# Two graph attention layers: the last products of each layer rearranged, the overflow count moved into layer 1, one early load moved forward

## The chip, the cores and the metric

The kernel runs on one core of a Trainium2 chip. The metric is the device time of one execution in microseconds (us), lower is better; the figure for a kernel is the median of its runs. Profiles are one execution each, taken by the hardware profiler. A core has five engines with a queue of instructions each: TensorE (PE, with its weight loads PEld), VectorE (DVE), ScalarE (ACT), GpSimd (POOL) and SyncE (SP). An engine works its queue off in order; engines wait for each other on semaphores.

## The reference

There are 2708 nodes with 1024 features each, `x`, and an adjacency matrix `adj` with some 16 entries that count in each row. Two layers follow each other, each with a residual and a layer norm without weights:

```python
# layer 0
f = x @ Wf + bf;  g = x @ Wg + bg
e = relu(f @ g.T)
attention = softmax(where(adj > 0, e, NEG), axis=1)
x = layernorm(x + attention @ (x @ W + bW))
# layer 1
h = x @ W1;  f1 = h @ a1;  f2 = h @ a2
e = leaky_relu(f1 + f2.T, 0.2)
attention = softmax(where(adj > 0, e, NEG), axis=1)
x = layernorm(x + relu(attention @ h))
```

## The kernel before

**Lists.** The first 225 us read `adj` and make of each row a list of its at most 40 neighbours, in four columns of up to 10 (`SL`). The nodes are sorted by the length of their lists into 85 groups of 32, and the groups stand in 22 blocks: block 0 has one group (20 valid nodes), the others four each (128 nodes). The table `TILES` says how many gathers each group gets, 3 to 10; a tile is one gather of 128 rows: for 32 nodes, one neighbour of each of the four columns. Over all groups there are 405 tiles. If a node of the input has more neighbours than its group has tiles for, the lists don't fit, and the kernel must take another path; that is what the overflow table `over` is for: it marks the places of `SL` beyond each group's tiles, and a valid neighbour in a marked place sets `flag`. The flag is loaded into the engines' registers at the end (`values_load`, L1065), and a branch (L102) jumps to `general_path` if it is set. With this input it is not.

**Reordered algebra.** Layer 0 takes M = Wf Wg^T once, so that the score of a node and its neighbour is a dot of the row `F = x M` with the neighbour's own `x`. The neighbours' `x` are gathered, weighted sums are made of them, and only then the sum is multiplied by `W` (`Wt`). Layer 1 likewise: it gathers rows of a table T, which holds the layer norm's output and beside it, in column D, that row's product with `u2 = W1 a2`; its score needs no dot, only that column and `f1`.

**A block in layer 0** (loop over `units`, in the order 1, 0, 2, 3, ..., 21). `lay.gathers` (L645) issues indirect DMAs on POOL into a ring of 20 slots, as soon as a slot is free. `f_product` is 32 matmuls of 128x512 and two short ones for the bias, on PE (`product`, L533, and `half_product`, L541). `replicate` copies F on ACT into the four `Fr` tiles. `dots` makes one DVE instruction with 1024 elements a tile. `soft` (L806 and L652) is the softmax on DVE, with its exponential on ACT; it ends with `st`, the weights spread for PE, and `rs`, the row sums. `sums` (L682) runs the weighted sums on PE into the PSUM tile `po`, whose scaled copy is `y`. `turn` (L515) transposes y on PE in eight steps, yields, and then copies the transposes on ACT to `yT`. `product` with `Wt` makes the last matrix product of the block in a PSUM tile `pm`. `close` (L817) adds the residual, computes mean and variance and three Newton steps for the inverse root on DVE (`norm`, L585), scales on ACT, stores the rows to X1S (SP), makes the two dots with `u1b` and `u2b` on DVE and scatters the row with its extra column into T (POOL). `load_residual` (L811) gathers the block's own x into the tile `zs`, which there is once; for the last block it goes into a ring slot.

The work is staggered over the loop: in the turn of block b, PE runs the sums of b, then the product of the block before with `Wt`, then F of a block ahead, then the transposes of y of b; the closing of the block before that is spread over the same turn as a generator of four pieces. All these engines are wrapped in `InOrder`, so program order is queue order. The PSUM pool `ps_m` has two buffers, each of two banks of 512 columns: F and the products with `Wt` take turns in them.

**Layer 1** goes over blocks 0 to 21 in that order with a ring of 32 slots (`ring` and `more`). Its turn has gathers from T, scores (`scores1`), softmax, sums, transposes, a product with `M`, now W1, and `close1` (L1001): relu, residual from X1S, norm, scatter to the output. After the loop come the last product, two closings, and then the overflow table: 88 memsets on POOL, three DVE instructions, a matmul and a copy to `flag`.

**At the start** x of block 1 and 0 and the lists of these blocks are gathered first, then the 15 tiles of block 1 (`lay.most`, L846), then x of block 2 (`load_x(2)`), then further lists.

Of the kernel before, what the change touches and what calls it, by code (L numbers as in the profile page):

```python
# [8 lines left out]
F32 = mybir.dt.float32  # L9
# [97 lines left out]
def listed_path(ctx, tc, x, adj, Wf, bf, Wg, bg, W, bW, W1, a1, a2, out):  # L107
# [433 lines left out]
    def half_product(pm, h, n, xT, w, row=None):  # L541
# [3 lines left out]
        for k in range(KC):  # L545
            pe.matmul(pm[:n, h, :], xT[:, k, :n], w[:, k, c],
                      start=(row is None and k == 0), stop=(k == KC - 1))

    def split_product(xT, w, parts, row=None):

        pm = ps_m.tile([P, H, 512], F32, name="pm")
        for h in range(H):
            c = slice(h * 512, (h + 1) * 512)
            if row is not None:
                pe.matmul(pm[:32, h, :], ones3[row:row + 3, :32], rows3[row:row + 3, c], start=True, stop=False)
            for k in range(KC // Q):
                for p in range(Q):
                    i = p * KC // Q + k  # L560
                    pe.matmul(pm[32 * p:32 * p + 32, h, :], xT[:, i, :32], w[:, i, c],
                              start=(k == 0 and (row is None or p > 0)), stop=(k + 1 == KC // Q))
        act.copy(parts, flat(pm))
        yield
        pm = ps_m.tile([P, H, 512], F32, name="pm")
        for h in range(H):
            pe.matmul(pm[:, h, :], rep, parts[:, h * 512:(h + 1) * 512], start=True, stop=True)
        return pm
# [13 lines left out]
            out=table, out_offset=bass.IndirectOffsetOnAxis(ap=idx, axis=0), in_=src,  # L582
            in_offset=None, bounds_check=N - 1, oob_is_err=False)

    def norm(z, n):  # L585


        st = small.tile([P, H, 6], F32, name="bst")
        mv = small.tile([P, 2], F32, name="mv")
        for h in range(H):  # L590
            dve.bn_stats(st[:n, h, :], z[:n, h * 512:(h + 1) * 512])
        dve.bn_aggr(mv[:n], st[:n])
        var, r, t = (small.tile([P, 1], F32, name=s) for s in ("var", "rstd", "newton"))
        dve.tensor_scalar(var[:n], mv[:n, 1:2], EPS, None, op0=ALU.add)
        ri, ti = r.bitcast(I32), t.bitcast(I32)
        dve.tensor_scalar(ti[:n], var.bitcast(I32)[:n], 1, None, op0=ALU.logical_shift_right)
        dve.tensor_scalar(ri[:n], ti[:n], -1.0, float(0x5F3759DF), op0=ALU.mult, op1=ALU.add)
        for _ in range(3):
            dve.tensor_scalar(t[:n], var[:n], r[:n], r[:n], op0=ALU.mult, op1=ALU.mult)
            dve.tensor_scalar(t[:n], t[:n], -0.5, 1.5, op0=ALU.mult, op1=ALU.add)  # L600
            dve.tensor_scalar(r[:n], r[:n], t[:n], None, op0=ALU.mult)
        sh = small.tile([P, 1], F32, name="sh")
        dve.tensor_scalar(sh[:n], mv[:n, 0:1], r[:n], -1.0, op0=ALU.mult, op1=ALU.mult)
        yield
        act.activation(z[:n, :D], z[:n, :D], AF.Identity, bias=sh[:n], scale=r[:n])
# [141 lines left out]
    with ExitStack() as s0s:  # L747
# [69 lines left out]
        def close(b):  # L817

            n, m, z = nrows[b], valid[b], Z.pop(b)
            dve.tensor_add(z[:n, :D], flat(Wp.pop(b))[:n], z[:n, :D])  # L820
            steps = norm(z, n)
            next(steps)
            yield
            for _ in steps:
                pass
            sp.dma_start(X1S[start[b]:start[b] + m, :], z[:m, :D])
            yield
            dot(z[:n, :D], u1b, n, f1[:n, b:b + 1])
            dot(z[:n, :D], u2b, n, z[:n, D:D + 1])
            yield  # L830
            if z is not zs:
                pool.memset(z[:, D + 1:], 0.0)
            scatter(T1[:, :], ids[:m, b:b + 1], z[:m])
# [9 lines left out]
        load_lists(0)  # L843
        q_dot(1)
        q_dot(0)
        lay.most = len(units[0].tiles)  # L846
        first_gathers(1, 5)
        x_turn(1)
        spread0, spread1 = q_spread(0), q_spread(1)
        next(spread1)  # L850
        load_x(2)
        load_lists(2)
        lay.most += len(units[1].tiles)
        first_gathers(0, 1)
        x_turn(0)

        halves, xT = [], xTs.pop(1)
        for h in range(H):
            halves.append(ps_m.tile([P, H, 512], F32, name="pm"))
            half_product(halves[h], h, P, xT, M, 0)  # L860
        pool.memset(zs[:, D:], 0.0)
        load_lists(3)
        next(spread0)
# [27 lines left out]
        for k, u in enumerate(units):  # L891
# [18 lines left out]
            next(closing, None)  # L910
            for r in reps[1:3]:
                replicate(nxt.b, r)
            lay.sums(u, po, {12: [lambda s=closing: [None for _ in s]]}, y[b])
            closing = iter(())
            if ahead is not None and not first:
                x_turn(ahead)
            if k + 3 < NB and not first:
                loaded = seq[k + 3]
                load_x(loaded)
            if back is not None:  # L920
                load_residual(back)
                if back > 0:
                    Wp[back] = product(P, yTs.pop(back)[0], Wt, 32)
                else:
                    Wp[back] = whole(split_product(yTs.pop(back)[0], Wt, frp.tile([P, D], F32, name="Fr"), 32))
# [11 lines left out]
            steps = turn(y[b], nrows[b], yT, halves=True)  # L937
            next(steps)
            yTs[b] = yT, steps
            if k + 4 < NB and not first:  # L940
                load_lists(seq[k + 4])
            if nxt is not None:
# [9 lines left out]
        load_residual(b)  # L952
        for _ in yTs[b][1]:
            pass
        Wp[b] = product(nrows[b], yTs.pop(b)[0], Wt, 32)
        for _ in closing:
            pass
        for _ in close(b):
# [3 lines left out]
    with ExitStack() as s1s:  # L962
# [38 lines left out]
        def close1(b):  # L1001
            m, xt, z = valid[b], x1[b % 2], z1[b % 2]
            sp.dma_start(xt[:m], X1S[start[b]:start[b] + m, :])
            dve.scalar_tensor_tensor(z[:m], flat(prod.pop(b))[:m], 0.0, xt[:m], op0=ALU.max, op1=ALU.add)
            for _ in norm(z, m):
                pass
            yield
            scatter(out, ids[:m, b:b + 1], z[:m])

        lay.gathers()  # L1010
        scores1(units[0])
        closing = iter(())
        waiting = []
        for k, u in enumerate(units):
            nxt = units[k + 1] if k + 1 < len(units) else None
            b = u.b
            back = b - 1 if b > 0 else None
            po = ps_s.tile([P, H, 512], F32, name="po")
            y[b] = yp.tile([P, D], F32, name="y1")
            if back is not None:  # L1020
                for _ in yTs[back][1]:
                    pass
            lay.sums(u, po, {6: [lambda s=closing: [None for _ in s]]}, y[b])
            closing = iter(())
            if back is not None:
                if back > 0:
                    prod[back] = product(P, yTs.pop(back)[0], M)
                else:
                    prod[back] = whole(split_product(yTs.pop(back)[0], M, z1[1]))
            yT = tp.tile([P, KC, P], F32, name="yT")  # L1030
            steps = turn(y.pop(b), nrows[b], yT, halves=True)
            next(steps)
            yTs[b] = yT, steps
            if waiting:
                closing = close1(waiting.pop())
                next(closing)
            if back is not None:
                waiting.append(back)
            if nxt is not None:
                scores1(nxt)  # L1040
        for _ in closing:
            pass
        b = NB - 1
        for _ in yTs[b][1]:
            pass
        prod[b] = product(nrows[b], yTs.pop(b)[0], M)
        for b in waiting + [b]:
            for _ in close1(b):
                pass


        over = ovp.tile([P, NG, QT], F32, name="over")
        pool.memset(over, 0.0)
        for g in range(1, NG):
            if TILES[g] < QT:
                pool.memset(over[:, g, TILES[g]:], 1.0)
        for q in range(Q):
            pool.memset(over[32 * q:32 * q + valid[0], 0, TILES[0]:], 1.0)
        dve.scalar_tensor_tensor(over, SL, float(N), over, op0=ALU.is_lt, op1=ALU.mult)
        dve.tensor_reduce(bad[:, 0:1], over, AX.XY, ALU.add)  # L1060
        dve.tensor_reduce(bad[:, 0:1], bad, AX.X, ALU.add)
        pt = ps_t.tile([P, 4, P], F32, name="pt")
        pe.matmul(pt[0:1, 0, 0:1], bad[:, 0:1], ones, start=True, stop=True)
        act.copy(flag, pt[0:1, 0, 0:1])
    return nc.values_load(flag[0:1, 0:1])  # L1065


@with_exitstack
def general_path(
# [360 lines left out]
```

## Time and profile before

| | us |
|---|---|
| median of 3 runs | 1803.02 |
| lowest, highest | 1797.66, 1807.29 |
| span of the profiled execution | 1799.5 |
| lists, and the first gathers of x | 0 to about 228 |
| layer 0, first matmul of a block to the last scatter to T | 228 to 1177 |
| layer 1, first gather from T to the last scatter of the output | 1177.6 to 1786.4 |
| overflow table, flag and the end of the program | 1786.4 to 1799.5 |

Busy over the whole span: PE 1573.3 us (87%), DVE 1172.8 (65%), POOL 1187.0 (66%), ACT 636.4 (35%). These shares are means over stages with different limits. A line of the timeline reads: start in us from the span's start, length in us, engine, line of the kernel (L71 is the wrapper `InOrder`, so nearly all lines name it; go by the tiles), operation, output tile <- input tiles, shape, how many were merged, and in brackets the engine's idle time ahead of it and what ended that. In a table by stage each engine's busy time stands with its count. POOL's 0.3 us between two DMA issues is shown as idle time that "issue" ended.

### The profile page before, as it was taken

How to read it: one execution, taken by the hardware profiler on the slowest of the kernel's cores; microseconds unless marked ns; L12 is line 12 of the kernel's file. 1: busy time of each engine (PE TensorE's matmuls, PEld its weight loads, DVE VectorE, ACT ScalarE, POOL GpSimd, SP SyncE). 2: the span in 40 equal slices, each digit the busy share in tenths (PEclk: the TensorE clock that was granted, in tenths of full speed). 3: DMA queues.
4: the chain of work that ended last, by engine and by line, in shares of the span. 5: the costliest groups of instructions: out<-in, count | busy, mean ns of one | idle time of the engine just before them, and what ended most of it. 6: DMA issues, size and time to landing. Idle time of an engine off the chain costs nothing. (4 is left out here: it accounts for less than half of the span.)

```text
span 1799.5 us, 22910 instructions
## 1 busy us (share of the span) xinstructions
PE 1573.3 (87%) x7313; PEld 669.9 (37%) x7313; DVE 1172.8 (65%) x3537; ACT 636.4 (35%) x861; POOL 1187.0 (66%) x1191
## 2 busy tenths in 40 slices
PE   5999279899999999999999997828989889889995
PEld 3544124343444443444444443303333333333332
DVE  4879737888888888888888887422442433433442
ACT  5545354444445545445554444101111111111110
POOL 7888476567666666766666653067777777777741
PEclk9999679899999999999999998959999999999997
DMA  7747068568777777777777786189999999999960
GB/s 267 262 151 261 20 238 303 209 211 292 292 262 263 261 262 260 278 276 287 289 293 275 260 292 227 71 339 368 362 394 393 393 360 396 392 391 381 370 229 26
DMA packets 149982, 501.86 MB, mean 279 GB/s; under 512 B 32565, under 2 KB 32597, under 8 KB 147144
## 3 DMA queue, kind: packets, MB, share of 16 engines
q0 software_dynamic: 132032, 427.36, 64.2%
q1 hardware_dynamic: 10202, 55.72, 8.2%
q10 hardware_dynamic: 7618, 17.23, 2.7%
q8 instruction: 59, 0.97, 0.2%
q14 instruction: 71, 0.58, 0.1%
HBM read 509.64 MB, written 33.75 MB: 302 GB/s over the span
## 5 line engine op out<-in xcount | busy, mean ns | idle before, releaser
L71 POOL DMA_INDIRECT ring<-in_x_dram,SL x405 | 439.9, 1086 | 258.2 <-issue 97.9
L71 DVE SCALAR_TENSOR_TENSOR j<-ring,Fr 128x1024 bf16<-128x1024 f32 x402 | 495.2, 1232 | 81.8 <-DMA ring<-in_x_dram,SL 55.6
L71 ACT COPY Fr<-pm 32x1024 f32<-32x1024 f32 (+2 forms) x353 | 340.7, 965 | 21.0 <-PE pm L71 16.3
L71 PE MATMUL po<-ring,st 128*32 128x512 f32 x2660 | 340.6, 619 | 0.1
L71 POOL DMA_INDIRECT ring<-T,SL x260 | 259.4, 998 | 84.9 <-issue 57.2
L71 PE MATMUL pm<-M,xT 128*128 128x512 f32 (+1 forms) x704 | 311.5, 622 | 0.4 <-ACT xT L71 0.4
L71 PE MATMUL pm<-Wt,xT 128*128 128x512 f32 (+1 forms) x704 | 303.5, 599 | 0.0
L71 PE MATMUL pm<-M,yT 128*128 128x512 f32 (+1 forms) x704 | 298.5, 595 | 0.3 <-ACT yT L71 0.3
L71 ACT ACTIVATE scores<-scores 128x24 f32<-128x24 f32 (+5 forms) x44 | 9.8, 222 | 667.7 <-DVE scores L71 667.7
L71 PEld LDWEIGHTS pm<-M,xT 128*128 128x128 f32 (+1 forms) x704 | 127.3, 191 | 172.1 <-issue 171.4
L71 PEld LDWEIGHTS pm<-M,yT 128*128 128x128 f32 (+1 forms) x704 | 127.2, 186 | 170.2 <-issue 169.7
L71 PEld LDWEIGHTS pm<-Wt,xT 128*128 128x128 f32 (+1 forms) x704 | 125.0, 186 | 151.8 <-issue 151.6
L71 POOL DMA_INDIRECT more<-T,SL x145 | 144.7, 998 | 44.6 <-issue 32.6
L71 PEld LDWEIGHTS po<-ring,st 128*32 128x32 f32 x2660 | 104.9, 115 | 185.6 <-issue 182.4
L71 DVE TENSOR_SCALAR scores<-ring,f1q 128x2 f32<-128x2 f32 (+5 forms) x98 | 21.7, 241 | 209.9 <-DMA ring<-T,SL 208.3
L409 POOL TENSOR_TENSOR adj<-adj,iota 128x2708 f32<-128x2708 f32 (+3 forms) x23 | 130.5, 5686 | 21.5 <-ACT adj L71 21.4
L71 ACT ACTIVATE y<-po,ri 128x512 f32<-128x512 f32 (+1 forms) x88 | 55.9, 684 | 221.4 <-PE po L71 203.9
L412 DVE MAX8 cand<-adj 128x8 f32<-128x136 f32 (+2 forms) x440 | 96.6, 285 | 36.3 <-POOL adj L409 36.3
L71 PE MATMUL pt<-rs,stack 128*32 128x1 f32 x680 | 13.8, 177 | 118.0 <-DVE rs L71 68.8
L71 PE MATMUL pm<-halfT,WfT 128*128 128x512 f32 x256 | 112.5, 594 | 1.5 <-ACT WfT L71 1.5
L71 POOL DMA_INDIRECT SL<-LD,idq x85 | 86.0, 1012 | 25.8 <-issue 20.9
L71 PE MATMUL po<-more,st 128*32 128x512 f32 x580 | 91.7, 639 | 0.0
(198 smaller groups left out, 1411.9 us busy)
## 6 DMA issues: line engine op xcount, KB each, us to landing
adj<-in_adj_dram SPq DMA_DIRECT2D x21, 1354.0 KB, 6.0
X1S<-z SPq DMA_DIRECT2D x20, 512.0 KB, 6.3
ring<-in_x_dram,SL POOLq DMA_INDIRECT x405, 6.4
u1b<-X1S SPq DMA_DIRECT2D x11, 512.0 KB, 7.1
rb<-X1S SPq DMA_DIRECT2D x10, 512.0 KB, 7.2
ring<-T,SL POOLq DMA_INDIRECT x260, 7.3
rows<-in_L_gnn_Wg_dram ACTq DMA_DIRECT2D x8, 512.0 KB, 6.4
rows<-in_L_gnn_Wf_dram ACTq DMA_DIRECT2D x8, 512.0 KB, 3.4
```

What stands on the lines that cost most here:

```text
L71: made = self.tc.keep_in_program_order(op(*args, **kwargs))
L409: nc.gpsimd.tensor_tensor(k[:n, cut], k[:n, cut], iota[:n, cut], op=ALU.mult)
L412: nc.vector.max(cand[:n, s, :], k[:n, s * SEG:min((s + 1) * SEG, N)])
```

## The change

It has four parts, all about the ends of the layers and one about the beginning.

1. Layer 0, last turn: the product of block 20 with `Wt` is queued ahead of the last sums instead of after them. For that its yT is copied out at the end of turn 20 already, ahead of the softmax of block 21 on ACT's queue, and what is left of the closing of block 19 and the residual of block 20 come first. The purpose is to give PE work while it waits for the last softmax.
2. The last product of both layers goes into two PSUM tiles of the pool instead of one, so that the add and the statistics of the first 512 columns can run while PE makes the second. In `close` the dot with `u2b`, which the scatter needs, is put ahead of that with `u1b`.
3. The overflow table is filled, eight memsets a turn, during the first eleven turns of layer 1; it is counted in the turn of block 12, and the flag is loaded at the end of the turn of block 20. It is to leave nothing but the branch for the end of the kernel.
4. At the start, x of block 2 is gathered after half of the tiles of block 1, so that the work on it can start sooner.

```diff
+    def two_products(n, xT, w, row=None):
+        halves = [ps_m.tile([P, H, 512], F32, name="pm") for h in range(H)]
+        for h in range(H):
+            half_product(halves[h], h, n, xT, w, row)
+        return halves
...
-    def norm(z, n):
+    def norm(z, n, made=None):
...
         for h in range(H):
+            if made is not None:
+                made(h)
             dve.bn_stats(st[:n, h, :], z[:n, h * 512:(h + 1) * 512])
...
         def close(b):
-            dve.tensor_add(z[:n, :D], flat(Wp.pop(b))[:n], z[:n, :D])
-            steps = norm(z, n)
+            pm = Wp.pop(b)
+            def add(h):
+                c = slice(h * 512, (h + 1) * 512)
+                dve.tensor_add(z[:n, c], pm[h][:n, h, :], z[:n, c])
+            if b + 1 < NB:
+                dve.tensor_add(z[:n, :D], flat(pm)[:n], z[:n, :D])
+            steps = norm(z, n, None if b + 1 < NB else add)
...
+            dot(z[:n, :D], u2b, n, z[:n, D:D + 1])
             dot(z[:n, :D], u1b, n, f1[:n, b:b + 1])
-            dot(z[:n, :D], u2b, n, z[:n, D:D + 1])
...
-        lay.most = len(units[0].tiles)
+        lay.most = len(units[0].tiles) // 2
         first_gathers(1, 5)
...
         load_x(2)
+        lay.most = len(units[0].tiles)
+        lay.gathers()
         load_lists(2)
...
+            if nxt is None:
+                for _ in closing:
+                    pass
+                load_residual(back)
+                Wp[back] = product(P, yTs.pop(back)[0], Wt, 32)
             lay.sums(u, po, {12: [lambda s=closing: [None for _ in s]]}, y[b])
...
-            if back is not None:
+            if back is not None and nxt is not None:
                 load_residual(back)
...
             yTs[b] = yT, steps
+            if k + 2 == NB:
+                for _ in steps:
+                    pass
...
-        Wp[b] = product(nrows[b], yTs.pop(b)[0], Wt, 32)
+        Wp[b] = two_products(P, yTs.pop(b)[0], Wt, 32)
...
         lay.gathers()
+        pool.memset(over, 0.0)
         scores1(units[0])
...
+            if k == NB // 2 + 1:
+                count_over()
             lay.sums(u, po, {6: [lambda s=closing: [None for _ in s]]}, y[b])
...
+            for i in (2 * k, 2 * k + 1):
+                if i < NB:
+                    mark_over(i)
+            if k + 2 == NB:
+                unfit = nc.values_load(flag[0:1, 0:1])
...
-        prod[b] = product(nrows[b], yTs.pop(b)[0], M)
+        prod[b] = two_products(P, yTs.pop(b)[0], M)
```

`close1` gets the same `add(h)` as `close`, with its relu in it; `mark_over(b)` holds the memsets of a block's groups, and `count_over` the three DVE instructions, the matmul and the copy to `flag` that stood at the end. The old block at the end is gone.

More of the change, by code (lines that the diff above doesn't have):

```diff
@@ L855, in listed_path @@
         x_turn(0)
[L857 to L860, printed above, removed]
+        halves = two_products(P, xTs.pop(1), M, 0)
         pool.memset(zs[:, D:], 0.0)
@@ L1003, in close1, with add @@
             sp.dma_start(xt[:m], X1S[start[b]:start[b] + m, :])
-            dve.scalar_tensor_tensor(z[:m], flat(prod.pop(b))[:m], 0.0, xt[:m], op0=ALU.max, op1=ALU.add)
-            for _ in norm(z, m):
+            pm = prod.pop(b)
+            def add(h):
+                c = slice(h * 512, (h + 1) * 512)
+                dve.scalar_tensor_tensor(z[:m, c], pm[h][:m, h, :], 0.0, xt[:m, c], op0=ALU.max, op1=ALU.add)
+            if b + 1 < NB:
+                dve.scalar_tensor_tensor(z[:m], flat(pm)[:m], 0.0, xt[:m], op0=ALU.max, op1=ALU.add)
+            for _ in norm(z, m, None if b + 1 < NB else add):
                 pass
@@ L1008, in close1, with mark_over, count_over @@
             scatter(out, ids[:m, b:b + 1], z[:m])
+        over = ovp.tile([P, NG, QT], F32, name="over")
+        def mark_over(b):
+            for g in groups[b]:
+                if g == 0:
+                    for q in range(Q):
+                        pool.memset(over[32 * q:32 * q + valid[0], 0, TILES[0]:], 1.0)
+                elif TILES[g] < QT:
+                    pool.memset(over[:, g, TILES[g]:], 1.0)
+        def count_over():
+            dve.scalar_tensor_tensor(over, SL, float(N), over, op0=ALU.is_lt, op1=ALU.mult)
+            dve.tensor_reduce(bad[:, 0:1], over, AX.XY, ALU.add)
+            dve.tensor_reduce(bad[:, 0:1], bad, AX.X, ALU.add)
+            pt = ps_t.tile([P, 4, P], F32, name="pt")
+            pe.matmul(pt[0:1, 0, 0:1], bad[:, 0:1], ones, start=True, stop=True)
+            act.copy(flag, pt[0:1, 0, 0:1])
         lay.gathers()
+        pool.memset(over, 0.0)
         scores1(units[0])
@@ L1049, in listed_path @@
                 pass
[L1052 to L1065, printed above, removed]
+    return unfit
 @with_exitstack
```

## The prediction

> **What bounds the kernel now.** I read four views, in this order: the page's list of costly groups, to see which engine is full where; the busy table by stage; and then the instructions in order of time at the three places that the change touches (start of layer 0, seam between the layers, end of the kernel).
>
> First, the stages. Columns: stretch, its length, busy time of PE, PEld, DVE, ACT and POOL with counts, granted clock, DMA share, GB/s.
> ```profile
> 282.00:1111.00 829.00, 795.12 (x3556) 335.86 (x3556) 713.79 (x1600) 414.92 (x499) 544.29 (x509) 0.99 0.75 269
> 1111.00:1178.00 67.00, 41.31 (x155) 16.47 (x154) 32.94 (x93) 7.48 (x12) 6.56 (x8) 0.81 0.26 93
> 1178.00:1705.00 527.00, 449.96 (x2541) 185.37 (x2542) 193.60 (x813) 69.72 (x135) 403.13 (x405) 0.94 0.99 381
> ```
> Layer 0 (first row) is TensorE: 795 of 829 us. The seam (second row) is 67 us in which nothing is full: a chain. Layer 1 (third row) looks like DMA (0.99), but 403 us of POOL in 405 instructions are 1.0 us each, and 0.30 us of issue lie ahead of each: 405 x 1.30 = 526 us of 527. So POOL's gather issue has no free slot there, and the DMA queue behind it is full too. The groups of that stage show the 0.30 us: 245 gathers, 77.9 us idle before them.
> ```profile
> L71 POOL DMA_INDIRECT ring<-T,SL x245 | 244.2, 997 | 77.9 <-issue 50.9 <-DMA ring<-T,SL 9.8 <-PE po L71 3.7
> ```
> Second, the seam in order of time (start, length, engine, what, idle time before and its releaser):
> ```profile
> 1110.07 1.04 PE L71 MATMUL pt<-ident,y 128*128 128x128 f32 x8
> ...
> 1121.05 0.22 ACT L71 ACTIVATE scores<-scores 128x16 f32<-128x16 f32 x1 [13.56 <-DVE scores L71]
> 1121.29 1.14 ACT L71 COPY xT<-pt 128x512 f32<-128x512 f32 x3
> ...
> 1122.25 0.39 PE L71 MATMUL pt<-rs,stack 128*32 128x1 f32 x16 [11.14 <-DVE rs L71]
> ...
> 1122.46 9.90 PE L71 MATMUL po<-ring,st 128*32 128x512 f32 x60
> ...
> 1136.12 1.03 POOL L71 DMA_INDIRECT z<-in_x_dram,ids  x1 [2.65 <-DMA T<-z,ids]
> ...
> 1147.16 1.23 DVE L71 TENSOR_TENSOR z<-pm,z 128x1024 f32<-128x1024 f32 x1 [15.41 <-PE pm L71]
> ...
> 1162.79 1.22 DVE L71 TENSOR_TENSOR ring<-pm,ring 128x1024 f32<-128x1024 f32 x1 [5.98 <-PE pm L71]
> ...
> 1173.37 1.00 POOL L71 DMA_INDIRECT T<-ring,ids  x1 [14.63 <-DVE fq L71]
> ...
> 1177.61 1.03 POOL L71 DMA_INDIRECT ring<-T,SL  x1 [3.24 <-DMA T<-ring,ids]
> ```
> The reader is to see that PE stands still for 11.14 us before the last sums while the transposed y of block 20 lies ready in PSUM, that its copy out waits behind the softmax on ACT's queue, and that two products of 14.8 us then follow the sums one after the other. The first gather of layer 1 hangs on the end of that chain.
>
> Third, the end of the kernel:
> ```profile
> 1778.00 1.23 DVE L71 SCALAR_TENSOR_TENSOR z<-pm,u1b 128x1024 f32<-128x1024 f32 x1 [9.38 <-PE pm L71]
> ...
> 1785.39 0.97 POOL L71 DMA_INDIRECT out_dram<-z,ids  x1 [14.25 <-ACT z L71]
> 1786.36 4.18 POOL L71 MEMSET over<- 128x850 f32 x88
> ...
> 1793.25 0.15 ACT L71 CAST flag<-pt 1x1 int32<-1x1 f32 x1 [8.13 <-PE pt L71]
> ```
> Last, the start, where x of block 2 is used:
> ```profile
> 254.96 0.58 PE L71 MATMUL pm<-rows,ones 3*32 3x512 bf16 x1 [9.21 <-ACT Fr L71]
> ...
> 255.33 1.23 DVE L71 SCALAR_TENSOR_TENSOR j<-xb,rb 128x1024 bf16<-128x1024 f32 x1 [9.32 <-DMA xb<-in_x_dram,ids]
> ...
> 281.56 0.31 PE L71 MATMUL pt<-rs,stack 128*32 128x1 f32 x16
> ```
>
> [...] after the 11.14 us gap the clock is 0.5 until 1128.2, and the 60 sums take 9.90 us where 64 take 7.05 us at 1088.42. [...] 1.0 us of POOL for each gather, so POOL work in layer 1 is not free. [...] the flag's loads take 0.46 to 0.54 us here.
>
> **Part by part.**
>
> x of block 2 sooner. Its gather (248.98) goes ahead of 8 of the 15 gathers of unit 0, 8 x 1.3 = 10.4 us. DVE's first dots can start when ACT's copies of Fr are there, about 250.2, not 256.97: DVE is 6.8 us earlier. But PE waits at 254.96 for ACT's copies, then runs the small product, the transposes and the product of block 2 without a pause to 281.35, and the sums follow at 281.56; rs was ready at 280.25. So the gain lies beside PE: **0** (0 to 1).
>
> Product of block 20 ahead of the last sums, with its y copied out early. Block 21's own case shows transposes to product as 1146.96 to 1147.93 = 0.97 us, so product 20 starts at 1111.0 and ends 14.8 us later, 1125.9. Its PSUM buffer was F of block 21, free since 1107.5. rs of unit 21 is ready at 1122.1, hence the sums start at 1125.9, at full clock: 60 x 0.110 + 0.4 = 7.0, end 1132.9. Now y, transposes and copies of block 21 are bare, as product 20 no longer hides them: unit 0 shows 289.17 to 291.24 = 2.1 us. Product 21 runs from 1135.0 to 1149.8, in place of 1162.75.
>
> Two PSUM tiles, and the other queue. The second half of product 21 takes the buffer that DVE's add of block 20 empties, a new wait. That add needs x in z, whose gather follows the scatter of block 19. With u2b's dot first, that scatter goes 1.27 us sooner: 1131.2; gather 3.7 later, 1134.9; landing 4.2 later (as at 1136.12), 1139.1; the add is over at 1140.4, the first half of product 21 at 1142.4. The wait is covered by 2 us. DVE goes on with block 20: add to shift 5.8 us (1147.16 to 1153.0), ACT 1.3, two dots 2.5: 1148.7. Then the halves of block 21, 0.62 + 0.65 each: the first is hidden until 1150.0, the second ends at 1151.3. Before, 1165.3: **14.0 us**. The dots' order gives the last scatter another **1.3** (it waits for u2b's dot at 1172.5, now the first of two). A 2 us pause of PE sometimes brings 3.4 us at half clock (after 710.83 it did, after 416.22 not): minus 0.5. Seam: **14.8** (8 to 15.5).
>
> Overflow table in layer 1. Its 88 memsets start 0.035 us apart (84 and more in 2.9 us), the first, of the whole table, takes 0.83. They now go in groups of 8 between gathers, on the full queue. A memset after a gather was seen at 260.39: 0.12 us, and the next gather started 1.32 us after the last one, not 1.30, so a single one fits into the gap. Eight take 0.35, so 0.25 too much: 11 x 0.25 + 0.7 for the first = 3.4 us. Low end 0, if the DMA queue paces (landing takes 6 to 9 us there, and 3.4 for a lone scatter, so it holds a backlog that swallows short pauses). High end: each memset costs a gap of 0.30. I take **2.7 lost**. The count (DVE 2.3 us ahead of the sums of block 12, PE's matmul behind it) delays those sums; PE was idle 1.6 to 3.9 us before most sums and the freed slots are wanted about 5 us later: nothing. The register load on five queues is 0.5 us, at block 20, after POOL's last gather: nothing.
>
> End. Between the end of the last scatter's issue (1786.36) and the branch on the flag (1794.0, after loads at 1793.43) 7.6 us go; the 5.5 us after the branch stay. The split of the last product saves one add and one stats, 0.62 + 0.65 = 1.3. The scatter lands some 3.4 us after issue, before the closing work is over. **8.9** (6.5 to 9.5).
>
> Sum: 14.8 + 8.9 - 2.7 = 21.0; 1803.0 - 21.0 = **1782**.
>
> **Rivals.**
> (A) DMA, not POOL, paces layer 1, and the memsets cost nothing: 1803.0 - 14.8 - 8.9 = 1779. For: DMA share 0.99 and the backlog. Against: POOL never misses a slot.
> (B) The wait moves to the residual: if the gather of x for block 20 takes 11.6 us, as the ring gather of 1100.48 did, DVE's add comes 7.4 us later and everything behind it: 1782 + 7.4 = 1789. Against: the queue is quiet then (93 GB/s), and the same gather took 4.2.
> (C) Slower: each of the 88 memsets costs 0.30 us between gathers, 26.4 + 0.8 = 27.2: 1803 - 14.8 - 8.9 + 27.2 = 1806. Against: the 0.12 us memset at 260.39.
> (D) Half of the seam and half of the end are lost to closing waits: 1803 - 7.4 - 4.5 + 2.7 = 1794, no change by the measure of 0.5% (9 us).
>
> **How the numbers follow.** Forecast 0.60, A 0.17, B 0.13, C 0.04, D 0.06. Forecast, A and B are faster by over 0.5%: 0.90; D the same 0.06; C slower 0.04. The range takes in A and B with the runs' own spread of 5 us about the median: 1774 to 1791.
>
> **What would show it.** In the profile after: PE idle before the last sums of layer 0 under 1 us and product 20 ahead of them; the first gather from T near 1163; no PE wait inside product 21; between the first gather from T and the last some 555 us, against 552 before; no memsets after the last scatter, and about 6 us from it to the end of the span. Wrong it would be if layer 1 stretched by more than 5 us, or if the first gather from T moved by less than 10.

## The result

| | median us | lowest to highest |
|---|---|---|
| before | 1802.09 | 1797.66 to 1807.29 (5 runs) |
| changed | 1788.55 | 1786.11 to 1790.74 (5 runs) |

The ratio is 0.9926, with a 95% interval of 0.9902 to 0.9950: faster by 0.5 to 1.0%. The gain of 13.5 us is less than the 20 to 21 us forecast; the time lies inside the range of 1774 to 1791.

**By stage.** One profile of each, measured between the same instructions:

| stretch | before | changed | gain | forecast |
|---|---|---|---|---|
| start to the first gather of x (code not changed) | 218.46 | 224.10 | -5.64 | 0 |
| to the first sums of unit 0 | 63.10 | 63.16 | -0.1 | 0 |
| to the transposes of y of block 20 | 828.51 | 828.72 | -0.2 | 0 |
| to the last scatter to T | 63.30 | 48.56 | 14.7 | 14.8 |
| to the first gather from T | 4.24 | 6.56 | -2.3 | 0 |
| first to last gather from T | 551.73 | 553.05 | -1.3 | -2.7 |
| to the last scatter of the output | 56.05 | 55.51 | 0.5 | 1.3 |
| to the end | 14.13 | 8.68 | 5.5 | 7.6 |

The first row is not the change's: in all the profiles of this study, whatever the kernel, it lies between 218.46 and 224.27 us. Without it the rows add up to 16.8 us, within the 9 to 18 us that the interval allows. The rows show where the forecast's other 4 us are missing: behind the last scatter to T, and at the end. In the row before last, two things meet: from the end of the last product to the scatter the change gains 1.1 us (7.5 and 6.4), and PE's work between the last gather and the end of that product took 0.6 us longer in this execution.

The table by stage of the changed kernel (columns as in the prediction):
```profile
287.00:1117.00 830.00, 797.45 (x3576) 336.93 (x3574) 713.96 (x1601) 415.28 (x500) 541.99 (x509) 0.99 0.74 269
1117.00:1171.00 54.00, 38.60 (x155) 15.57 (x154) 33.10 (x94) 7.19 (x12) 8.20 (x7) 0.91 0.32 114
1171.00:1700.00 529.00, 457.36 (x2539) 185.50 (x2540) 195.96 (x816) 68.64 (x134) 406.75 (x492) 0.92 0.98 379
```
Only the middle row has changed much: 54 us in place of 67, granted clock 0.91 in place of 0.81. In the third, POOL has 492 instructions, 87 more, for 3.6 us more of busy time.

The seam in order of time:
```profile
1115.98 1.04 PE L71 MATMUL pt<-ident,y 128*128 128x128 f32 x8
...
1117.27 7.13 PE L71 MATMUL pm<-Wt,xT 128*128 128x512 f32 x16
...
1131.71 0.30 PE L71 MATMUL pt<-rs,stack 128*32 128x1 f32 x16
...
1131.86 7.05 PE L71 MATMUL po<-ring,st 128*32 128x512 f32 x60
...
1141.20 1.03 POOL L71 DMA_INDIRECT z<-in_x_dram,ids  x1 [3.13 <-DMA T<-z,ids]
1141.24 7.13 PE L71 MATMUL pm<-Wt,xT 128*128 128x512 f32 x16
...
1145.57 1.23 DVE L71 TENSOR_TENSOR z<-pm,z 128x1024 f32<-128x1024 f32 x1 [8.30 <-DMA z<-in_x_dram,ids]
...
1155.14 0.68 DVE L71 TENSOR_TENSOR ring<-pm,ring 128x512 f32<-128x512 f32 x1
...
1157.18 0.69 DVE L71 BATCH_NORM_STATS2 bst<-ring 128x6 f32<-128x512 f32 x1
...
1164.55 1.34 POOL L71 DMA_INDIRECT T<-ring,ids  x1 [8.32 <-DVE j L71]
...
1165.05 0.33 SPq L71 DMA_DIRECT2D u1b<-X1S  x1
...
1171.11 1.03 POOL L71 DMA_INDIRECT ring<-T,SL  x1 [5.22 <-DMA T<-ring,ids]
```
The 11.14 us of PE's wait are gone: the last sums have no idle time ahead of them, and run in 7.05 us, at a granted clock of 1.00 (1131.8 to 1139), in place of 9.90, where the clock was 0.50 until 1128. DVE's add of block 20 waits 8.30 us for x, whose gather in turn had to wait for the scatter of block 19 out of the same tile `z`; the add still comes before the second half of product 21 needs the buffer (it ends at 1146.80, and that half starts at 1148.62), but it makes DVE late for block 21. But look at the last three lines. A load from X1S now starts half a us after the last scatter, and the first gather from T waits 5.22 us for that scatter to land, where it waited 3.24.

The end:
```profile
1773.35 0.69 DVE L71 SCALAR_TENSOR_TENSOR z<-pm,u1b 128x512 f32<-128x512 f32 x1 [5.39 <-PE pm L71]
...
1779.67 0.98 POOL L71 DMA_INDIRECT out_dram<-z,ids  x1 [13.11 <-ACT z L71]
```
And of the changed kernel's transfers in its last 15 us, the one issue: transfer, queue, count, us from issue to landing.
```profile
out_dram<-z,ids POOLq DMA_INDIRECT x1, 4.5
```
Nothing follows the scatter any more, yet 8.68 us go to the end of the span: 4.5 of them are the scatter's own way to memory, and 4.2 pass after that. That the landing is waited for shows in POOL's queue: of its closing waits on semaphores, one lasts from 1780.76 to 1784.22, and the scatter landed at 1784.19. In the kernel before the same wait, at 1794.75, took 0.04 us.

The experiments ran later, on the chips numbered 0 and 3; on which chip the two kernels of this section ran, the "first pair" below, is not on record. In the experiments every kernel, the kernel before too, has a median of 1970 to 2050 us, and the kernel before alone went from 1999.9 to 2033.8 us between two groups of runs on chip 0. So their stretches are compared rather than their times.

### The profile page after: what moved, and what is told of

It reads as the page before. It is cut to its first block, busy times and chain, and to the rows that moved or that the text cites. A ratio compares the mean times of both kernels' runs of the same rounds, so it can differ in the third digit from the quotient of the medians.

```text
span 1788.3 us, 22916 instructions
## 1 busy us (share of the span) xinstructions
PE 1584.4 (89%) x7313; PEld 671.7 (38%) x7313; DVE 1173.5 (66%) x3539; ACT 637.3 (36%) x861; POOL 1186.7 (66%) x1191
## 5 line engine op out<-in xcount | busy, mean ns | idle before, releaser
L71 PE MATMUL po<-ring,st 128*32 128x512 f32 x2660 | 344.9, 622 | 0.1
L71 ACT ACTIVATE y<-po,ri 128x512 f32<-128x512 f32 (+1 forms) x88 | 55.9, 684 | 237.1 <-PE po L71 212.0
L71 PE MATMUL po<-more,st 128*32 128x512 f32 x580 | 97.6, 668 | 0.0
L71 PE MATMUL pt<-rs,stack 128*32 128x1 f32 x680 | 13.9, 178 | 94.4 <-DVE rs L71 56.9
```

The source lines that it names most:

```text
L71: made = self.tc.keep_in_program_order(op(*args, **kwargs))
```

## The experiments

**What is different in these runs.** PE in layer 1, in a run of the changed kernel (label a1_after; start, length, idle time ahead):
```profile
1366.02 0.59 PE L71 MATMUL pm<-M,yT 128*128 128x512 f32 x1 [0.84 <-issue]
1368.18 0.59 PE L71 MATMUL pm<-M,yT 128*128 128x512 f32 x1 [1.58 <-issue]
1370.29 1.01 PE L71 MATMUL pm<-M,yT 128*128 128x512 f32 x1 [1.51 <-issue]
```
Inside a product, with nothing to wait for, matmuls start up to 2 us apart for about 11 us, and this comes back every 34 to 36 us; the two profiles of the first pair have no such pause in these products. Why it is so is open: both chips show it, and the chip of the first pair is not known. The mean granted clock is 0.90 to 0.92 (0.948 in the changed kernel's first profile). Layer 0 takes 35 to 95 us longer, and layer 1 changes its bound. POOL's wait for PE's sums ahead of gathers into `ring`, in the same run (us in total, times, longest),
```profile
POOL ring L71 <- PE po L71: 63.1, 16, 11.3
```
was 4.0 us in total in the kernel before of the first pair. The gathers now wait for PE's sums to free slots. The seam and the end of the kernel are short chains that mostly fall between these pauses, and repeat to half a us: over five runs that share it, the seam takes 55.5 to 55.9 us.

**Theory 1**: the seam's gain is that of product 20 ahead of the sums. The two tiles in layer 0, x of block 2 and the order of the dots bring nothing. The order even costs time: the load into `u1b`, which layer 1 issues early for its x of block 1, has to wait for the dot that reads `u1b`; with that dot last, the load starts beside the last scatter. At the end, the landing of the last scatter takes the place of the overflow table. **Rivals**: the tiles or the order carry part of the seam's gain; the slower landing is a matter of chance or of the earlier scatter; DMA and not POOL is what makes layer 1 longer by 1.3 us.

**1. The changed kernel and the kernel before again** (labels a1_after on chip 0, b1_before on chip 3; no edit).

> The changed kernel itself, once more, as the measure of the others of this group and of how much the first stage, the lists, moves from one execution to the next. Theory 1 (the 5.6 us by which the lists took longer in the first profile are chance): the first gather of x starts somewhere between 218 and 225 us, and the kernel stays 10 to 17 us faster than before. Theory 2 (the change slows the lists): the first gather starts at 224 again and not earlier.

> The kernel before, for its stretches on the same chip. Theory 1: transposes of y of block 20 to the first gather from T 66 to 67.5 us, from the last scatter of the output to the end 14.1, first to last gather from T as in the run of the product alone.

Measured: the first gather of x starts at 218.75 us in the changed kernel and at 224.27 in the kernel before, the other way round than in the first pair: the 5.6 us are not the change's. The changed kernel takes 2008.40 us, ratio 0.9972 (0.9931 to 1.0014), so a gain of 10 us is neither shown nor excluded by the times here; the single run of the kernel before took 2037.1. From the transposes of y of block 20 to the first gather from T: 55.56 against 66.08, in the first pair 55.12 against 67.54. The 1.4 us between the two executions of the kernel before are its last sums, 8.49 us in place of 9.90 (7.05 in the changed kernel at clock 1.00), after an idle time of 11.03 us in place of 11.14; at what clock they ran is not shown. From the last scatter of the output to the end: 8.18 against 14.06. So the parts to be taken apart are there in these runs as well, while the gain in time is mostly lost in the spread.

**2. The product ahead, alone** (label e10_product_alone). Everything else reverted: products in one tile, dots in the old order, x of block 2 late, table at the end. Of its edits, the two at the seam:
```diff
-            dot(z[:n, :D], u2b, n, z[:n, D:D + 1])
             dot(z[:n, :D], u1b, n, f1[:n, b:b + 1])
+            dot(z[:n, :D], u2b, n, z[:n, D:D + 1])
...
-        Wp[b] = two_products(P, yTs.pop(b)[0], Wt, 32)
+        Wp[b] = product(P, yTs.pop(b)[0], Wt, 32)
```


> Of the changed kernel only the product of block 20 ahead of the last sums is kept; one PSUM tile, the old order of the dots, x of block 2 late, table at the end. Theory 1 (the seam's gain is that of the product, the two tiles bring about half a us since DVE is busy with the dots of block 20, and the new order of the dots brings nothing): transposes of y of block 20 to the last scatter 49 to 51 us, on to the first gather from T 4.2, together 53.5 to 55 (changed kernel 55.1 to 55.6); from the last scatter of the output to the end 14.1. On a chip where POOL paces layer 1 the time between first and last gather from T is that of the kernel before, 551 to 552. Rival (the two tiles or the order carry several us of the seam): together 58 us or more.

Measured: 50.52 us to the last scatter, 54.88 to the first gather, 14.21 at the end. PE in this kernel:
```profile
1209.86 1.04 PE L71 MATMUL pt<-ident,y 128*128 128x128 f32 x8
...
1211.14 7.13 PE L71 MATMUL pm<-Wt,xT 128*128 128x512 f32 x16
...
1225.74 7.05 PE L71 MATMUL po<-ring,st 128*32 128x512 f32 x60
```
The same order and the same 7.05 us as in the changed kernel. This one part takes the seam from 66.08 to 54.88, 11.2 us, on the same chip; all the parts together reach 55.56 (chip 0). The rival's 58 is out. The kernel's time says nothing (2031.25 us; ratio 1.0034, 0.9841 to 1.0227).

**3. One tile instead of two** (label e9_one_tile). Both last products in one PSUM tile, all else as changed.
```diff
-        Wp[b] = two_products(P, yTs.pop(b)[0], Wt, 32)
+        Wp[b] = product(P, yTs.pop(b)[0], Wt, 32)
...
-        prod[b] = two_products(P, yTs.pop(b)[0], M)
+        prod[b] = product(P, yTs.pop(b)[0], M)
```


> The last products of both layers in one PSUM tile again, all else as changed. Theory 1: transposes of y of block 20 to the first gather from T 55.6 to 56.3 us (changed kernel 55.1 to 55.6); from the sums of the last block to the last scatter of the output 1.1 to 1.3 us longer than in the changed kernel (66.1 against 64.95). Where POOL paces layer 1: first to last gather from T 552.5 to 554, as in the changed kernel (553.05). Rival (two tiles are worth 1.3 us or more in each layer): 56.9 or more at the seam.

Measured: 55.63 at the seam (55.5 to 55.9 with two tiles): nothing. DVE's add of block 21, in one piece, has hardly to wait for product 21:
```profile
1213.97 1.23 DVE L71 TENSOR_TENSOR ring<-pm,ring 128x1024 f32<-128x1024 f32 x1 [0.16 <-PE pm L71]
```
At the end of layer 1 the two differ cleanly. The last product and the scatter with one tile:
```profile
1967.60 14.00 PE L71 MATMUL pm<-M,yT 128*128 128x512 f32 x32 [0.29 <-ACT yT L71]
...
1989.08 0.98 POOL L71 DMA_INDIRECT out_dram<-z,ids  x1 [14.24 <-ACT z L71]
```
and with two, in the run a1_after:
```profile
1975.61 14.00 PE L71 MATMUL pm<-M,yT 128*128 128x512 f32 x32 [0.29 <-ACT yT L71]
...
1995.97 0.97 POOL L71 DMA_INDIRECT out_dram<-z,ids  x1 [13.12 <-ACT z L71]
```
From the end of the product, 1981.60 to 1989.08 = 7.48 us against 1989.61 to 1995.97 = 6.36: two tiles are worth 1.12 us here. In layer 0 they are worth nothing, because DVE is still at block 20 until 1155.14 of the seam shown above, when both halves of product 21 are nearly done (its second half ends at 1148.62 + 7.13 = 1155.75). DVE is that late because it waited 8.30 us for x of block 20; whether the two tiles would pay with that x loaded earlier, no run shows. The time of this kernel: 2032.25 us, ratio 1.0032 (0.983 to 1.0235).

**4. The order of the dots back** (label e1_dots_back).
```diff
-            dot(z[:n, :D], u2b, n, z[:n, D:D + 1])
             dot(z[:n, :D], u1b, n, f1[:n, b:b + 1])
+            dot(z[:n, :D], u2b, n, z[:n, D:D + 1])
```


> The changed kernel with the dot with u1b ahead of that with u2b again. Theory 1 (the early scatter is given back): issued while DVE is still at the second dot, the scatter takes POOL 1.3 to 1.9 us instead of 1.0, and the load of x into u1b, freed only by the last dot, now runs beside the scatter, so that it lands after 5.7 us instead of 3.4. With the old order the last scatter to T starts about 1.3 us later but takes 1.0 us and lands after about 3.4, so from the transposes of block 20 to the first gather from T it is 53 to 55 us (55.1 in the changed kernel): no slower, 0 to 1.5 us faster. Theory 2 (the prediction's step): the order of the dots is worth 1.3 us, so this stretch becomes 56.4 us and the kernel 1.3 us slower.

Measured: 50.61 to the last scatter (48.91 in the changed kernel), from there 4.18 to the first gather (6.65), together 54.78. In five runs with the new order and the load as changed it is 55.5 to 55.9. So with the new order the scatter goes 1.7 us sooner, and the first gather still comes 0.7 to 1.1 us later. The SP queue's load and POOL's two lines with the old order:
```profile
1220.61 0.33 SPq L71 DMA_DIRECT2D u1b<-X1S  x1
...
1222.73 1.00 POOL L71 DMA_INDIRECT T<-ring,ids  x1 [8.75 <-DVE fq L71]
...
1226.90 1.03 POOL L71 DMA_INDIRECT ring<-T,SL  x1 [3.18 <-DMA T<-ring,ids]
```
Of the 1.7 us, 1.4 are the order's: from the last statistics of block 21 (the BATCH_NORM_STATS2 in the seam above) to the scatter it is 8.03 us in all five profiles with the old order and 6.67 with the new. Time: 1987.92 us, ratio 0.9907 (0.9852 to 0.9962).

**5. The load out of the way** (label e2_load_elsewhere). In layer 1 the free tile takes x of block 1, and `u1b` becomes an output tile, so that the early load waits for no dot.
```diff
-        x1 = [rb, u1b]
-        z1 = [u2b, zp.tile([P, D], F32, name="z1")]
+        x1 = [rb, zp.tile([P, D], F32, name="z1")]
+        z1 = [u2b, u1b]
```


> The changed kernel with two tiles of layer 1 exchanged: the residual x of odd blocks is loaded into a fresh tile instead of u1b, and their norm works in u1b. The load for block 1 then has no dot to wait for. Theory 1 (the load beside the scatter delays the landing): the load is issued right behind that for block 0, ahead of the scatter, and the scatter to first gather stretch falls from 6.6 us to between 4.2 and 5.2. Theory 2 (it is DVE's dot, or a matter of this one execution, that delays the landing): it stays above 6 us.

Measured: 49.06 to the scatter, 4.92 on to the gather, together 53.98; time 1971.77 us, ratio 0.9824 (0.9754 to 0.9894). The 6.6 fell to 4.9 with the order of the dots kept, and e7 and e11 below, which have the same edit, show 4.98 and 4.89. So most of it is the load, and neither chance nor the order as such. Its SP queue:
```profile
1211.59 0.36 SPq L71 DMA_DIRECT2D rb<-X1S  x1
1212.06 0.49 SPq L71 DMA_DIRECT2D z<-X1S  x1
```
and its scatter and first gather on POOL:
```profile
1213.25 1.34 POOL L71 DMA_INDIRECT T<-ring,ids  x1 [8.32 <-DVE j L71]
1218.17 1.03 POOL L71 DMA_INDIRECT ring<-T,SL  x1 [3.58 <-DMA T<-ring,ids]
```
The second load is issued 1.2 us ahead of the scatter; in the changed kernel it came 0.5 us behind it, and in the kernel before 2.1 us ahead (1171.25 to 1173.37). POOL waits about 3.6 us for the landing, not 5.22. What stays over the old 4.2 is for one half POOL's own issue, 1.34 us where it was 1.00, and for the other the wait for the landing, 3.58 us where it was 3.24.

**6. x of block 2 late again** (label e4_x2_back).
```diff
-        lay.most = len(units[0].tiles) // 2
+        lay.most = len(units[0].tiles)
...
         load_x(2)
-        lay.most = len(units[0].tiles)
-        lay.gathers()
```


> The changed kernel with x of block 2 gathered after all 15 tiles again. Theory 1 (prediction): the sums of the first unit start as long after the first gather of x as before, 63.1 us, within 0.3 us, because PE is bound by ACT's copies of Fr; DVE's softmax of that unit is some 4 to 7 us later than in the changed kernel, which nobody sees; time the same. Theory 2: the early load shortens the start, and without it the sums start 1 us or more later.

Measured: the softmax's sums `rs` of unit 0 are ready 61.20 us after the first gather of x, against 56.9 with the early load (in the kernels of parts 4 and 5, run beside it); the first sums on PE start after 69.69 against 70.1. The early load makes DVE some 4 us earlier and brings nothing on PE. Time 1985.03 us, ratio 0.9931 (0.9890 to 0.9972).

**7. The table: moved alone, and not moved** (labels e5_table_alone, e6_no_table). The first has the table in layer 1 and the other parts reverted: the edits of parts 3, 4 and 6, and
```diff
-            if nxt is None:
...
-                Wp[back] = product(P, yTs.pop(back)[0], Wt, 32)
...
-            if back is not None and nxt is not None:
+            if back is not None:
```
with which the product of block 20 follows the last sums again (the early copy of its yT goes too). The second is the changed kernel with the table at the end:
```diff
-        pool.memset(over, 0.0)
         scores1(units[0])
...
+        pool.memset(over, 0.0)
+        for i in range(NB):
+            mark_over(i)
+        count_over()
```


> The kernel before with the overflow table's part alone (memsets and count inside layer 1). Theory 1 (the end waits for the landing of the last scatter): from the last scatter's issue to the end of the span 8.4 to 8.8 us instead of 14.1, so 5.5 us gained, less 1 to 2 us for the memsets in the gathers: 3.5 to 5 us faster than before. Theory 2 (the prediction's step): 6.5 us from the last scatter to the end, 7.6 gained, less 2.7.

> The changed kernel with the overflow table at the end again. Theory 1: the seam alone, 12.4 us of the stretch from the transposes of block 20 to the first gather from T (67.5 to 55.1), and about 1 us at the last product; first gather to last gather 0.5 to 2 us shorter than in the changed kernel: 13 to 15 us faster than before in the stretches that the change touches. Theory 2 (the prediction's size of the seam): 14.8 us.

Measured, last scatter to the end: 8.47 with the table moved alone, 14.28 with all but the table, 8.18 changed, 14.06 before. The end's 5.6 to 6.1 us belong to the table's move; they come with and without the other parts. The times do not fit: e5 2046.95 us, ratio 1.0160 (1.0069 to 1.0251), where a gain was to be seen; e6 2027.63, ratio 1.0005 (0.9955 to 1.0055). But e5 was executed four times, at 2029 to 2060 us, and the kernel before 43 times beside it, at 1988 to 2073: all of e5 lies inside that spread. In e5 the stretch between first and last gather is 692.9 us, in the changed kernel 687.1, in the kernel before 684.1: there PE and not the gathers decides, and this stretch varies from 670 to 693 us over the runs, more from one group of runs to the next than with any of the edits. Whether this kernel is slower in these runs at all, and why, is open.

**8. The memsets off POOL, and the two edits together** (labels e3_memset_dve, e7_best, e11_best). e3 puts the table's memsets on DVE. e11 has that and the load out of the way. e7 has both and, for the last block, half of the scaling on DVE while ACT does the other half (the second group of lines, e7 alone).
```diff
-                    pool.memset(over[:, g, TILES[g]:], 1.0)
+                    dve.memset(over[:, g, TILES[g]:], 1.0)
...
-        act.activation(z[:n, :D], z[:n, :D], AF.Identity, bias=sh[:n], scale=r[:n])
+            act.activation(z[:n, :512], z[:n, :512], AF.Identity, bias=sh[:n], scale=r[:n])
+            dve.tensor_scalar(z[:n, 512:D], z[:n, 512:D], r[:n], sh[:n], op0=ALU.mult, op1=ALU.add)
```


> The changed kernel with the table's memsets on DVE instead of POOL. Theory 1 (POOL's issue paces layer 1): the 0.2 us after every group of eight and the 0.7 us after the first are gone, and first gather to last gather from T falls from 553.0 us to 550 to 552. Theory 2 (the DMA queue paces, and short pauses of POOL are made up for): it stays within 0.5 us of 553.

> The changed kernel with three edits that the theories ask for: the residual x of odd blocks of layer 1 goes into a fresh tile, the table's memsets run on DVE, and of the last norm of each layer ACT scales the first half of the row and DVE the second. Theory 1: 1.1 us of the transposes to first gather stretch for the tile, 0.5 us more for the halved scaling, 0.5 us at the very end, and where layer 1 is paced by POOL 1 to 2.4 us of its gathers for the memsets: 2 to 4.5 us in all. Theory 2 (POOL paces nothing, the DMA queue does): the stretch of the gathers stays as in the changed kernel, and only about 2 us come.

> The changed kernel with two edits: in layer 1 the tile of the early load of x and one of the output tiles are exchanged, so that the load doesn't wait for the dot with u1b and is over before the last scatter; and all memsets of the table stand on DVE. Theory 1 (the load beside the scatter costs 1.8 us, and the memsets cost issue slots of POOL, which paces layer 1): last scatter to first gather from T 4.2 to 5.0 (changed kernel 6.6); first to last gather from T 551 to 552 where POOL paces it, as without the table, against 553.05; time 2.5 to 4 us below the changed kernel, ratio to the kernel before about 0.990. Rival (DMA paces layer 1, and what is longer there is the DMA's own spread): first to last gather unchanged, 552.5 to 554.

Measured, first to last gather: e3 674.5, e7 693.3, e11 685.4, against 670.5, 674.3 and 676.9 in the other kernels beside e3, 686.9 to 692.9 beside e7, 683.0 to 685.6 beside e11. There is no difference, and none was to be expected: with POOL waiting 60.6 to 66.4 us for PE's sums ahead of gathers into `ring` (e9, e11, a1_after, b1_before), issue slots are free there. Whether POOL or DMA made layer 1 longer by 1.3 us in the first pair is not settled by these runs. The seam is 53.77 in e7 and 53.68 in e11, 1.9 below the changed kernel. The halved scaling shows where its stretch is taken alone: in e7 the last statistics of block 21 are followed by the scatter after 6.26 us (6.67 in the changed kernel), and the end of the last product of layer 1 by its scatter after 6.10 (6.35). So it brings 0.4 and 0.25 us, where 0.5 each was expected; over the seam as a whole, 53.77 against 53.68 without it, other differences hide it. Times: e3 1980.14 us, without an interval; e7 1997.23, ratio 0.9866 (0.9788 to 0.9945); e11 2020.86, ratio 1.0042 (0.9911 to 1.0173). A version better than the changed one is shown at the seam, by 1.9 us, but not in the time.

## Why the forecast was right, and by how much it was off

The direction was right, and the mechanism held for the largest term; the order of the dots and the end were counted too high. The time came to lie inside the range partly by luck. It is next to the 1789 of rival B, which did not happen, and the range was wide enough because B and A were let in (its upper end, by its own rule, should even have been 1789 + 5 = 1794). One of the signs of being wrong, read by the clock, did occur: the first gather from T moved from 1177.6 to 1171.1, less than 10 us. Only without the 5.6 us of the lists, which are not the change's, is it 12.1. And 8.7 us, not about 6, go from the last scatter to the end.

**Product 20 ahead: close to the forecast.** 14.0 us were worked out for it and the two tiles, up to the last statistics of block 21. In the kernel before these are
```profile
1164.05 1.29 DVE L71 BATCH_NORM_STATS2 bst<-ring 128x6 f32<-128x512 f32 x2
```
and end 55.27 us after the transposes of y of block 20; in the changed kernel they end after 41.89 (1157.18 + 0.69). That is 13.4. Product 20 alone is worth 11.2 us on chip 3, where the kernel before has 1.4 us less to lose in its last sums (8.49 us for 9.90): some 12.6 in the first pair, by that estimate. The clock is in that sum: without the 11.14 us of idle time ahead of them the sums run at a granted clock of 1.00 and take 7.05 us for 9.90. Rival B is out: DVE's add starts 4.4 us after the gather of x for block 20 was issued (1141.20), and product 21 has no wait inside. The chain of the residual ran as it was worked out.

**The two tiles**: in layer 1 1.12 us against 1.3 forecast. In layer 0 the working had DVE free 1.1 us before product 21 ends; it was free 0.6 us before in the first pair, and in the experiments between 0.5 us before and 0.1 us behind. That the halves then bring nothing (part 3) was not said.

**The dots' order: the step that failed.** "The dots' order gives the last scatter another 1.3": it did, from the last statistics to the scatter 8.0 us became 6.7. But the path does not end there. It ends with the first gather, and that came some 0.9 us later than with the old order (part 4). Two things were missed. First, the load into `u1b` is queued behind the dot with `u1b`; with that dot last, 512 KB go beside the scatter, which costs 1.7 us (part 5). The prediction asked who waits for `u2b` and not who waits for `u1b`. Second, POOL makes the scatter while DVE runs the other dot, which adds 0.3 us to the last scatter's issue. In the seam of the changed kernel the last three scatters take 1.87, 1.87 and 1.34 us; here are the last two with the dots beside them:
```profile
1153.99 1.23 DVE L71 SCALAR_TENSOR_TENSOR j<-z,u1b 128x1024 bf16<-128x1024 f32 x1
1154.23 1.87 POOL L71 DMA_INDIRECT T<-z,ids  x1 [10.71 <-DVE j L71]
...
1163.79 1.23 DVE L71 SCALAR_TENSOR_TENSOR j<-ring,u1b 128x1024 bf16<-128x1024 f32 x1
1164.55 1.34 POOL L71 DMA_INDIRECT T<-ring,ids  x1 [8.32 <-DVE j L71]
```
The dots end at 1155.22 and 1165.02, and POOL is done at 1156.10 and 1165.89: 0.88 and 0.87 us behind the dot's end, though one began 0.24 us and the other 0.76 us after the dot. It is no matter of these two. In the kernel before, 138 of POOL's 983 indirect DMAs begin inside one of DVE's dots, at least 0.05 us after its start and over 0.1 us before its end; all of them end 0.86 to 0.91 us after its end and take up to 2.04 us. The other 845 take 0.99 us in the median, among them 38 that begin within 0.03 us of a dot's start and take 0.99 to 1.01. With the order put back the scatter begins behind the dots and takes 1.00 us (part 4). What couples the two is not shown.

**The end: too large by 2.9 us.** 8.9 were forecast (7.6 + 1.3), and 0.5 + 5.5 came. The failed sentence is "the scatter lands some 3.4 us after issue, before the closing work is over". It was true with the table behind it, and taking the table away made it false: the landing, 4.5 us in this profile, is now waited for (3.46 us of POOL, where it was 0.04), and 4.2 us follow. The 3.4 us were those of the last scatter to T before; here the landing took 4.5. All kernels with the table moved end 8.1 to 8.7 us after their last scatter, and in the changed kernel's profile the landing is half of it: of the 14.1 us before, 5.5 could be had by moving the table, and not 7.6.

**The memsets: dearer than forecast, and made up for elsewhere.** 2.7 us were taken, below the 3.4 that had been worked out, and the stretch became 1.3 longer. The trace of the changed kernel shows each part (POOL, the first two groups, then a later one):
```profile
1211.34 0.99 POOL L71 DMA_INDIRECT more<-T,SL  x1 [0.31 <-issue]
1212.33 0.82 POOL L71 MEMSET over<- 128x850 f32 x1
1213.32 1.00 POOL L71 DMA_INDIRECT ring<-T,SL  x1 [0.16 <-issue]
...
1216.91 0.80 POOL L71 MEMSET over<- 20x7 f32 x8
1218.31 1.00 POOL L71 DMA_INDIRECT ring<-T,SL  x1 [0.59 <-issue]
...
1237.44 0.34 POOL L71 MEMSET over<- 128x6 f32 x7
1237.93 1.00 POOL L71 DMA_INDIRECT ring<-T,SL  x1 [0.15 <-issue]
```
Gathers start 1.30 us apart; here it is 1213.32 - 1211.34 = 1.98, so 0.68 lost to the large memset, 1.1 once at the first group, and 1237.93 - 1236.45 = 1.48, so 0.2 for each later group (0.25 was worked out; one of them lost 0.4). All together they come to 4.0 us. But the other delays between gathers, beyond 1.297 us each, fell from 5.9 to 3.2 us in sum, the longest from 2.3 us (before, at 1709.52) to 1.3 (at 1704.35), so that 1.3 is left. Whether the memsets shortened them or chance did is not shown; the small net loss may be luck. Rival C, 27 us, is out by this; A and the forecast stay untold apart.

**x of block 2: nothing, as forecast.** DVE's first dot over the neighbours starts 29.5 us after the first gather of x, before 38.5; it then waits once more for ACT's copies, and `rs` of unit 0 is ready after 53.8 us, before 61.8: 7.9 us sooner, where 6.8 was worked out. PE's wait for the copies of F ends 36.6 us after that gather, before 36.5.

## What to carry to other kernels

Follow a path to its last waiter: a scatter that is issued sooner has gained nothing until it has landed, and on the way it can meet a transfer that the same edit released later (here issued 1.7 us sooner, and the first gather came 0.7 to 1.1 us later). When the work after the last transfer is taken away, the transfer's landing becomes the end (here 3.46 us of waiting for 0.04); price what is left of it, not the work alone. Where the idle window of an engine also cost it the clock, as the 11.14 us did here (9.90 us of sums for 7.05), a product pulled into that window pays twice. Splitting a product's result in two paid 1.12 us in layer 1, and nothing in layer 0, where the consumer was not free when the first half was done.

## What the hardware showed besides

- The same two programs, run again later on chips 0 and 3, took some 200 to 230 us longer, with matmuls inside a product starting up to 2 us apart for about 11 us at a time. This moved the bound of layer 1 from the gathers (551.7 us) to PE (670 to 693 us), so an edit that saves gather slots can bring something in one set of runs and could bring nothing in the other. Whether the chip or something else made the difference is open.
- POOL's issue of one scatter of 128 rows took 1.00 us with no dot beside it and 1.87 with one that had begun 0.24 us before; the latter ended 0.88 us after the dot.
- The changed kernel ends with a scatter from POOL: 4.5 us from its issue to its landing and 4.2 us more to the end of the span.
